# An edge-gated graph layer on one core: transposed h loaded for two row blocks in one transfer, projected rows stored in one transfer of 4 KB packets

## The chip, the core and the metric

The kernel runs on one NeuronCore of a Trainium2 chip. The metric is the time of one execution on the device in microseconds (us), as the median of several runs. A kernel is a program for five engines that run side by side: TensorE (PE, matmuls; its weight loads are PEld), VectorE (DVE), ScalarE (ACT), GpSimd (POOL) and SyncE (SP), which does nothing but hand transfers to the core's 16 DMA engines. They are tied together by semaphores.

## The reference

With B = 16 graphs, N = 1024 nodes and D = 256 features, and one matrix `adj` that serves as both `A_a` and `A_m`:

```python
pre_u = einsum('bud,dk->buk', h, W1[:d]);  pre_v = einsum('bvd,dk->bvk', h, W1[d:])
hidden = relu(pre_u[:, :, None, :] + pre_v[:, None, :, :] + b1)
S   = sigmoid(einsum('buvk,ko->buvo', hidden, W2)[..., 0] + b2)
a_t = einsum('buv,bud->bvd', S * adj, h)
m_t = einsum('uv,bud->bvd', adj, h) * h
z   = beta1 * h + beta2 * (a_t @ Wa + ba) + beta3 * (m_t @ Wm + bm)
```

About 0.9% of `adj` is not zero (some nine entries in a column), so the kernel computes the gate S for these edges alone.

## The kernel before

The 16 graphs are four groups g of four graphs. The 1024 target nodes v are eight row blocks vt of 128. One block of the main loop is a pair (g, vt): 32 blocks, each of T = 10 steps, so 320 steps in all. In a step, 128 edge slots are worked on for the four graphs of g:

- POOL gathers for each slot one row of a table in HBM (`fetched<-table,uidx`, L512). A table row holds, for source node u and the group's four graphs, `pre_u` (1024 floats, the projected row) and beside it h itself (1024 floats), 8 KB together. There is one table per group. A gather takes one of eight places `fetched`, and is issued as soon as TensorE has used the step that was in that place.
- PE spreads `pre_v + b1` to the slots (`pc<-X,mark`, L621), DVE adds it (L652, one instruction a step, by which steps are counted in the trace) and forms the gate's sum (L659, four a step), ACT applies the sigmoid and scales, PE sums over the edges (L675).
- Every block ends with products with Wa and Wm (L746) and two stores of the result, `out_dram<-z` (L753; 256 KB each, 1 KB packets).

Beside this, the tables of the next groups are made while the current group runs. For each row block (g, nt) to come, SP copies h into the table's right half (`copy_h`, L404; 512 KB, 1 KB packets), and loads the transposed h, `hT` (L399; 512 KB, in packets of 512 bytes, since 128 nodes of one feature lie side by side). Then TensorE multiplies it with W1's upper half in two halves (`half_product`, L410), ACT copies each half to SBUF, and SP stores it to the left half of the table (L438; two stores of 256 KB, 2 KB packets). The two halves are made five steps apart: for (2, i) at steps 69+10i and 74+10i, for (3, i) at 149+10i and 154+10i. The same `hT` is read again when the block (g, nt) runs itself, for `pre_v` and for z, and its place is given back only then.

Places for `hT`: eight slices of one tile `wide` (they hold group 0 at the start), two tiles of their own, and from step 71 three more. `pending` lists the loads by the step at which the row block is needed; `made_rows` hands over the first of the list when a place is free and that step is at most AHEAD = 14 steps away. Row blocks (1, 6) and (1, 7) are loaded twice, since group 1's table begins with them (the list `again`; the second time for steps 130 and 140).

The order on every engine is the order of the code (the schedule is manual). SP's transfers are numbered over eight completion semaphores in turn, and each hand-over waits until the transfer eight before it has landed. Nothing can overtake on SP: a store that waits for ACT holds up the load behind it.

Of the kernel before, what the change touches and what calls it, by code (L numbers as in the profile page):

```python
# [7 lines left out]
FP = mybir.dt.float32  # L8
# [5 lines left out]
P = 128  # L14
# [3 lines left out]
def kernel(  # L18
# [42 lines left out]
    nc = tc.nc  # L61
    B, N, D = x.shape
    NT = N // P
    DC = D // P
    GB = 4
    NG = B // GB
    GD = GB * D
# [16 lines left out]
    table = [dram.tile([N, 2 * GD], FP, name=f"table{g}") for g in range(NG)]  # L84
    adj_flat = adjT.rearrange("v (u one) -> (v u) one", one=1)
    x_rows = x.rearrange("b n d -> n b d")
    xT_rows = xT.rearrange("b (c p) n -> p (b c) n", p=P)
# [6 lines left out]
    def load_weights(src, name, engine=nc.scalar):  # L94
        t = const.tile([P, DC, D], FP, name=name)
        engine.dma_start(t, src.rearrange("(c p) k -> p c k", p=P))
        return t
# [102 lines left out]
    big = main.enter_context(tc.tile_pool(name="big", bufs=2))  # L200
# [9 lines left out]
    def small(name):  # L210
        return psm.tile([P, 512], FP, name="misc")
# [158 lines left out]
    def after(step, f):  # L370
        due.setdefault(step, []).append(f)
# [6 lines left out]
    again = [(1, vt) for vt in range(NT - TWICE, NT)]  # L378
    hTs = {}
    NH = NT + 2  # L380

    def hT_places(pool, n, first=0):
        return [pool.tile([P, GB, DC, P], FP, name=f"hT{first + i}") for i in range(n)]

    wide = hts.tile([P, GB, DC, N], FP, name="wide")
    hT_free = hT_places(hts, NH - NT)
    flat = list(hT_free)

    def drop_hT(k, step=None):
        t = hTs.pop(k)  # L390
        if step is None:
            hT_free.append(t)
        else:
            after(step, lambda: hT_free.append(t))

    def load_hT(k, engine=nc.sync):
        g, nt = k
        hTs[k] = hT_free.pop(0)
        engine.dma_start(hTs[k].rearrange("p b c n -> p (b c) n"),  # L399
                         xT_rows[:, g * GB * DC:(g + 1) * GB * DC, nt * P:(nt + 1) * P])  # L400

    def copy_h(k, engine=nc.scalar):
        g, nt = k
        engine.dma_start(table[g][nt * P:(nt + 1) * P, GD:].rearrange("n (b d) -> n b d", b=GB),  # L404
                            x_rows[nt * P:(nt + 1) * P, g * GB:(g + 1) * GB, :])

    def half_product(p, hT, wt, h, begun):
        for bb in range(2):
            for i in range(DC):
                nc.tensor.matmul(p[:, bb * D:(bb + 1) * D], hT[:, 2 * h + bb, i, :], wt[:, i, :],  # L410
                                 start=(i == 0 and not begun), stop=(i == DC - 1), skip_group_check=begun)
# [7 lines left out]
    def copied(step, t, p):  # L419
        if ROOM <= step < BS * T - 4 and step % T in BEHIND or step == BS * T - 7:  # L420
            behind.append((t, p))
        else:
            nc.scalar.copy(t, p)  # L423

    def rows(k, tab=None):

        g, nt = k
        for h in range(2):
            step = yield
            c = slice(2 * h * D, (2 * h + 2) * D)  # L430
            p = small("p")
            half_product(p, hTs[k], w_u, h, False)
            t = big.tile([P, 2 * D], FP, name=f"tab{h}") if tab is None else tab[:, c]
            copied(step, t, p)
            if h == 1 and k in again:
                drop_hT(k, step + 1 if tab is None else None)
            if tab is None:
                after(step + 1, lambda t=t, c=c: nc.sync.dma_start(table[g][nt * P:(nt + 1) * P, c], t))  # L438
        if tab is not None:
            after(step + 1, lambda: nc.sync.dma_start(table[g][nt * P:(nt + 1) * P, :GD], tab))  # L440

# [41 lines left out]
    def do(step):  # L485
        for f in due.pop(step, ()):
            f()

    def go(gen, step):

        try:
            gen.send(step)
        except StopIteration:
            pass
# [2 lines left out]

    BS = NG * NT
    EVS = 3
    ROOM, MORE, LISTS, AHEAD = 10, 3, 70, 14  # L500
    BEHIND = (5, 6, 7, 8)
    APART, minus = 24, []

# [19 lines left out]
    tabs = [fetched[0][:, :GD], fetched[NF - 1][:, :GD], *(f[:, GD:] for f in fetched)]  # L523
    for nt in range(NT):
        hTs[0, nt] = wide[:, :, :, nt * P:(nt + 1) * P]
    for b in range(GB):
        nc.sync.dma_start(wide[:, b], xT_rows[:, b * DC:(b + 1) * DC, :])
        for vt in ((), (0, 1), (2,), (3,))[b]:
            next(made[vt])
# [15 lines left out]
    def load_mark(q):  # L545
        marks[q] = big.tile([P, E], FR, name="mark")
        nc.scalar.copy(marks[q], whose[:, order[q // NW][1] * NW + q % NW, :])
# [17 lines left out]
    for t, turns_ in enumerate(script):  # L565
        step = t - 100
        do(step)
        for c in turns_.split():
            if c == "r":
                k = turn[m % NT]  # L570
# [45 lines left out]
    def expand(n):  # L616
        k, g, vt, w, j = where(n)
        pcs[n] = psc.tile([P, GD], FP, name="pc")
        for h in range(2):
            c = slice(2 * h * D, (2 * h + 2) * D)  # L620
            nc.tensor.matmul(pcs[n][:, c], marks[n // TW][:, j * P:(j + 1) * P], cuts[k][w][:, c],  # L621
                             start=True, stop=True)
# [21 lines left out]
    def fill(n, gap=True):  # L644
        for r in running:
            if r[1] == gap and r[2] <= n:
                piece_of(r, n)
                break

    def add(n):  # L650
        t = fetched[at_slot[n]][:, :GD]
        nc.vector.tensor_tensor(t, t, pcs.pop(n), ALU.add)  # L652
# [109 lines left out]
    def tail_rows(t, v, m, f):  # L762
        g, vt = order[BS - 1]
        for i in range(P // m):
            b = g * GB + i + (f * P // m if m == W else 0)
            yield hbs[BS - 1][i * m:(i + 1) * m, f, :], t[b, vt * P + v:vt * P + v + m, :]
# [37 lines left out]
    at, pending = {}, []  # L804
# [14 lines left out]
    def made_rows(n):  # L819
        nonlocal piece, last  # L820
        while pending and (pending[0][1] in hTs or hT_free and pending[0][0] - (AHEAD if n >= T else 6) <= n):
            k = pending.pop(0)[1]
            if k not in hTs:
                load_hT(k, nc.sync)
        if n in at:
            if at[n] != last:
                last = at[n]
                copy_h(last, nc.sync)
                piece = rows(last)
                next(piece)  # L830
            go(piece, n)
# [46 lines left out]
    def pair_ends():  # L878
        while ends:
            pair_end(ends.pop(0))  # L880
# [3 lines left out]
    def gather_to(last_in):  # L884
        nonlocal done
        while done < min(last_in, total):
            gather_in(done)
            done += 1

    for n in range(total - 3):  # L890
        k, s = divmod(n, T)
        if n < ROOM:
            gather_to(n - 1)
        pair_ends()
        if n % TW == (n < ROOM) and n // TW + 1 < total // TW:
            load_mark(n // TW + 1)
        expand(n + 2)
        if n >= ROOM:
            fill(n, False)
        products(n, k, s)  # L900
        if n >= ROOM and n % 2 == 0:
            gather_to(n)
        add(n + 1)
        gate(n)
        while behind:
            nc.scalar.copy(*behind.pop(0))  # L906
        do(n)
        if n == 0:
            for i in advance[0]:
                next(made[i], None)  # L910
            next(made[EARLY])
            load_hT(turn[NT + 1])
            w_a, w_m = load_weights(Wa, "w_a", nc.sync), load_weights(Wm, "w_m", nc.sync)
            after(10, scale_weights)
        if n == total - 6:
            hbs[BS - 1] = next(t for t in hT_free if t in flat).rearrange("p b c n -> p b (c n)")
            for v, m, f in tails:
                for h, o in tail_rows(x, v, m, f):
                    nc.sync.dma_start(h, o)
        for i in advance.get(n, ()) if n else ():  # L920
            next(made[i], None)
        if n in start_list:
            running.append([made[start_list[n]], True, n])
            piece_of(running[-1], n)
        if n < ROOM:
            fill(n, False)
        if n == LISTS:
            assert not running and all(next(x, None) is None for x in made)
            lists_done()
            more = main.enter_context(tc.tile_pool(name="more", bufs=1))  # L930
            flat.extend(hT_places(more, MORE, NH))
            hT_free.extend(flat[-MORE:])
            minus.append(more.tile([P, P], FR, name="minus"))
            nc.vector.tensor_scalar(minus[0], ident, -1.0, None, ALU.mult)

    k, n = BS - 1, total - 3
# [45 lines left out]
    with tc.If(any_left > 0):  # L982
        with ExitStack() as s2:
# [4 lines left out]
            for vt in range(NT):  # L988
# [17 lines left out]
                f = fb.tile([P, 2 * GD], FP, name="fb_f")  # L1006
# [83 lines left out]
```

## Time and profile before

| | |
|---|---|
| runs | 1022.89, 1018.49, 1019.88 us; median 1019.88 us |
| profiled execution | 1017.41 us; span of its instructions 1015.6 us; granted TensorE clock 0.979 of full speed on average |
| share of the span | PE 94%, PE weight loads 69%, DVE 93%, ACT 87%, POOL 43% |
| transfers | 126622 packets, 373.95 MB, 368 GB/s on average |
| issued by SP, largest | 32 copies of h to the tables, 62 stores of z, 48 stores of projected rows, 26 loads of hT by L399 |

"Span" is the time from the first to the last instruction of the profiled execution. The shares say in which part of it an engine was busy. The page gives the DMA engines' work as the time that packets took, as a share of 16 engines over the span, by queue: q0 are POOL's gathers, q1 is what SP hands over.

### The profile page before, as it was taken

How to read it: one execution, taken by the hardware profiler on the slowest of the kernel's cores; microseconds unless marked ns; L12 is line 12 of the kernel's file. 1: busy time of each engine (PE TensorE's matmuls, PEld its weight loads, DVE VectorE, ACT ScalarE, POOL GpSimd, SP SyncE). 2: the span in 40 equal slices, each digit the busy share in tenths (PEclk: the TensorE clock that was granted, in tenths of full speed). 3: DMA queues.
4: the chain of work that ended last, by engine and by line, in shares of the span. 5: the costliest groups of instructions: out<-in, count | busy, mean ns of one | idle time of the engine just before them, and what ended most of it. 6: DMA issues, size and time to landing. Idle time of an engine off the chain costs nothing.

```text
span 1015.6 us, 21650 instructions
## 1 busy us (share of the span) xinstructions
PE 954.2 (94%) x6408; PEld 702.7 (69%) x6408; DVE 948.0 (93%) x3302; ACT 888.6 (87%) x2754; POOL 436.6 (43%) x441
## 2 busy tenths in 40 slices
PE   7878998988989999999799999999999999999996
PEld 5755766766767777777577777777777776666763
DVE  7589998989889999999889999999999999999994
ACT  3667988888979999999789999999999999999983
POOL 3166766556464334343333434333333344434430
PEclk9988998999999999999999999999999999999998
DMA  9899999889899999999999999999999999999992
GB/s 325 308 345 391 382 319 352 324 293 390 304 382 381 417 409 411 402 402 400 386 366 397 417 410 407 399 404 411 379 409 373 380 374 357 381 366 376 373 362 62
DMA packets 126622, 373.95 MB, mean 368 GB/s; under 512 B 17584, under 2 KB 81072, under 8 KB 90288
## 3 DMA queue, kind: packets, MB, share of 16 engines
q0 software_dynamic: 48640, 296.70, 74.6%
q1 hardware_dynamic: 77232, 75.26, 22.1%
q8 instruction: 53, 0.87, 0.3%
q10 hardware_dynamic: 624, 0.52, 0.2%
q14 instruction: 73, 0.60, 0.2%
HBM read 376.48 MB, written 50.33 MB: 420 GB/s over the span
## 4 chain that ended last, share of the span: by engine, by line
PE 59%; DVE 21%; ACT 6%; issue 6%; DMA 5%; another core or an unknown queue 0%; POOL 0%; SPq 0%; DVEq 0%; POOLq 0%
PE misc L410 18%; PE misc L746 11%; PE pc L621 11%; DVE fetched L659 11%; PE acc L675 10%; DVE fetched L652 8%; PE misc L697 5%; DMA wide<-in_xT_dram 4%; ACT left L666 2%; PE misc L730 2%; DVE LT L714 1%; PE misc L414 1%; DMA fetched<-table,uidx 1%; ACT X L906 1%; ACT ev L683 1%
## 5 line engine op out<-in xcount | busy, mean ns | idle before, releaser
L512 POOL DMA_INDIRECT fetched<-table,uidx x320 | 339.4, 1061 | 502.7 <-PE acc L675 372.4
L659 DVE SCALAR_TENSOR_TENSOR fetched<-fetched,w_b 128x256 f32<-128x256 f32 x1280 | 473.3, 418 | 0.0
L652 DVE TENSOR_TENSOR fetched<-fetched,pc 128x1024 f32<-128x1024 f32 x320 | 388.1, 1213 | 32.6 <-PE pc L621 22.8
L666 ACT ACTIVATE left<-left,gt 128x16 f32<-128x16 f32 x1280 | 285.9, 299 | 0.0
L621 PE MATMUL pc<-X,mark 128*128 128x512 f32 x640 | 228.8, 452 | 15.1 <-issue 7.4
L675 PE MATMUL acc<-fetched,left 128*32 128x256 f32 x2560 | 181.9, 387 | 5.0 <-issue 2.3
L621 PEld LDWEIGHTS pc<-X,mark 128*128 128x128 f32 x640 | 107.3, 190 | 97.9 <-issue 58.6
L675 PEld LDWEIGHTS acc<-fetched,left 128*32 128x32 f32 x2560 | 70.9, 109 | 79.9 <-issue 26.0
L746 PE MATMUL misc<-w_m,LT 128*128 128x256 f32 x496 | 117.6, 380 | 0.0
L746 PE MATMUL misc<-w_a,LT 128*128 128x256 f32 x496 | 117.4, 379 | 0.0
L662 ACT ACTIVATE gt<-sc,b_b 128x4 f32<-128x4 f32 x320 | 96.8, 302 | 13.8 <-DVE fetched L659 10.3
L746 PEld LDWEIGHTS misc<-w_a,LT 128*128 128x128 f32 x496 | 93.6, 189 | 14.3 <-ACT LT L423 0.2
L410 PE MATMUL misc<-w_u,wide 128*128 128x256 f32 x352 | 88.3, 402 | 15.2 <-DMA wide<-in_xT_dram 7.5
L683 ACT COPY ev<-acc 128x512 f32<-128x512 f32 x160 | 92.4, 577 | 11.1 <-remote 3.2
L353 POOL DMA_INDIRECT val<-in_adjT_dram,vidx x80 | 86.9, 1086 | 32.8 <-issue 20.8
L659 DVE DVE_READ_ACCUMULATOR fetched<-fetched,w_b 128x1 f32 x1280 | 100.9, 79 | 0.0
L629 ACT ACTIVATE left<-onehot,val 128x32 f32<-128x32 bf16 x320 | 100.3, 313 | 0.0
L746 PEld LDWEIGHTS misc<-w_m,LT 128*128 128x128 f32 x496 | 89.4, 190 | 10.1 <-issue 0.4
L697 PE MATMUL misc<-ident,ev 128*128 128x128 f32 x642 | 84.3, 276 | 9.7 <-ACT ev L683 4.3
L410 PE MATMUL misc<-w_v,wide 128*128 128x256 f32 x368 | 90.5, 390 | 0.0
L410 PEld LDWEIGHTS misc<-w_u,wide 128*128 128x128 f32 x352 | 70.0, 202 | 27.9 <-issue 8.1
L697 PEld LDWEIGHTS misc<-ident,ev 128*128 128x128 f32 x642 | 74.9, 142 | 20.7 <-ACT ev L683 5.2
(160 smaller groups left out, 996.4 us busy)
## 6 DMA issues: line engine op xcount, KB each, us to landing
table<-in_x_dram SPq DMA_DIRECT2D x32, 512.0 KB
out_dram<-z SPq DMA_DIRECT2D x62, 256.0 KB
table<-tab SPq DMA_DIRECT2D x48, 256.0 KB
wide<-in_xT_dram SPq DMA_DIRECT2D x15, 512.0 KB
hT<-in_xT_dram SPq DMA_DIRECT2D x11, 512.0 KB
fetched<-table,uidx POOLq DMA_INDIRECT x320
wide<-in_xT_dram SPq DMA_DIRECT2D x4, 1024.0 KB
table<-fetched SPq DMA_DIRECT2D x8, 512.0 KB
```

Of the source, the lines that this page charges most:

```text
L410: nc.tensor.matmul(p[:, bb * D:(bb + 1) * D], hT[:, 2 * h + bb, i, :], wt[:, i, :], start=(i == 0 and not begun), stop=(i == DC - 1), skip ...
L512: nc.gpsimd.indirect_dma_start(out=fetched[at_slot[n]], out_offset=None, in_=table[g], in_offset=bass.IndirectOffsetOnAxis(ap=uidx[:, vt * ...
L621: nc.tensor.matmul(pcs[n][:, c], marks[n // TW][:, j * P:(j + 1) * P], cuts[k][w][:, c], start=True, stop=True)
L629: nc.scalar.activation(lefts[n][:, 1::GB, :], onehot[:, vt * NW + w, j, :].unsqueeze(1).to_broadcast([P, GB // 2, V]), AF.Copy, scale=val[ ...
L652: nc.vector.tensor_tensor(t, t, pcs.pop(n), ALU.add)
L659: nc.vector.scalar_tensor_tensor(t[:, b, :], t[:, b, :], 0.0, w2_b, ALU.max, ALU.mult, accum_out=sc[:, b:b + 1])
L662: nc.scalar.activation(gt, sc, AF.Sigmoid, bias=b2_b)
L666: nc.scalar.activation(lefts[n][:, 2 * b, :], lefts[n][:, 1 + b // 2 * GB, :], AF.Copy, scale=gt[:, b:b + 1])
L675: nc.tensor.matmul(accs[i][b * 2 * V:(b + 1) * 2 * V, r, :], left[:, 2 * b - b % 2:2 * b - b % 2 + 2].rearrange("p k v -> p (k v)"), f[:, ...
L683: nc.scalar.copy(evs[i], accs.pop(i))
L697: nc.tensor.matmul(pt[:, :, FROM[j]:FROM[j] + V], evs[i][:, r, c * P:(c + 1) * P], ident, is_transpose=True, start=(j == of[0]), stop=True ...
L746: nc.tensor.matmul(pz[:, bb * D:(bb + 1) * D], LT[:, 2 * h + bb, i if bb else 1 - i, c, :], wt[:, c, :], start=(i == 1 and bb == 0 and c = ...
```

## The change

1. A twin is a tile whose two halves are two neighbouring places. The four neighbouring pairs of `wide` are twins, and of the three places added at step 71 two become one tile `both`, a fifth twin. Where the first load in `pending` has an even nt (and belongs to group 2 or 3, or is (1, 6)), and a twin is wholly free, `load_pair` loads (g, nt) and (g, nt+1) in one transfer of 1 MB, in packets of 1 KB.
2. Where no twin is free, such a load is put off (`break`) until SINGLE = 9 steps before its row block is needed, rather than 14, and is then a single load. What stands behind it in `pending` is put off with it.
3. `free_single` picks the place of a single load so that whole twins stay free if possible.
4. `rows` makes both halves of a projected row block in one tile `tab`, and stores it after the second half in one transfer of 512 KB in packets of 4 KB. For groups 2 and 3 the first half so leaves five steps later than before.

```diff
+    def load_pair(k, two):
+        g, nt = k
+        full = with_twin(two[0])
+        for i, t in enumerate(two):
+            hT_free[:] = [f for f in hT_free if f is not t]
+            hTs[g, nt + i] = t
+        nc.sync.dma_start(full.rearrange("p b c n -> p (b c) n"),
+                          xT_rows[:, g * GB * DC:(g + 1) * GB * DC, nt * P:(nt + 2) * P])
...
     def rows(k, tab=None):
         g, nt = k
+        own = tab is None
+        if own:
+            tab = big.tile([P, GD], FP, name="tab")
         for h in range(2):
             step = yield
             c = slice(2 * h * D, (2 * h + 2) * D)
             p = small("p")
             half_product(p, hTs[k], w_u, h, False)
-            t = big.tile([P, 2 * D], FP, name=f"tab{h}") if tab is None else tab[:, c]
-            copied(step, t, p)
+            copied(step, tab[:, c], p)
...
-            if tab is None:
-                after(step + 1, lambda t=t, c=c: nc.sync.dma_start(table[g][nt * P:(nt + 1) * P, c], t))
-        if tab is not None:
-            after(step + 1, lambda: nc.sync.dma_start(table[g][nt * P:(nt + 1) * P, :GD], tab))
+        after(step + 1, lambda: nc.sync.dma_start(table[g][nt * P:(nt + 1) * P, :GD], tab))
...
+    for nt in range(0, NT, 2):
+        twins.append((wide[:, :, :, nt * P:(nt + 2) * P], (hTs[0, nt], hTs[0, nt + 1])))
...
         while pending and (pending[0][1] in hTs or hT_free and pending[0][0] - (AHEAD if n >= T else 6) <= n):
-            k = pending.pop(0)[1]
+            t, k = pending[0]
+            other = next((e for e in pending if e[1] == (k[0], k[1] + 1)), None)
+            if k not in hTs and other and k[1] % 2 == 0 and (k[0] > 1 or k in again):
+                two = free_pair()
+                if two is None and t - SINGLE > n:
+                    break
+                if two is not None:
+                    load_pair(k, two)
+                    pending.remove(other)
+            pending.pop(0)
             if k not in hTs:
                 load_hT(k, nc.sync)
...
-            flat.extend(hT_places(more, MORE, NH))
-            hT_free.extend(flat[-MORE:])
+            flat.extend(hT_places(more, MORE - 2, NH))
+            hT_free.extend(flat[2 - MORE:])
+            both = more.tile([P, GB, DC, 2 * P], FP, name="both")
+            twins.append((both, (both[:, :, :, :P], both[:, :, :, P:])))
+            hT_free.extend(twins[-1][1])
```

In the built program only SP's order differs, apart from the names of the tiles. Of the 26 loads of hT, 22 stay single; the two pairs are (2,2)+(2,3) into `both` and (2,4)+(2,5) into `wide`. The 48 stores of halves become 24.

SP around steps 110 to 130, before. `hT_203` is the load of row block (2,6), `hT_204` the second one of (1,7), `wide` that of (2,7); the two copies `table_62<-in_x_dram` are those of (2,4) and (2,5):

```order
L404 DMA table_62<-in_x_dram 128x4x256
L438 DMA table_62<-tab_5176 128x512
L399 DMA hT_203<-in_xT_dram 128x8x128
L438 DMA table_62<-tab_5339 128x512
L399 DMA hT_204<-in_xT_dram 128x8x128
L753 DMA out_dram<-z 128x2x256 x2
L404 DMA table_62<-in_x_dram 128x4x256
L438 DMA table_62<-tab_5542 128x512
L399 DMA wide<-in_xT_dram 128x8x128
```

The same place now; the first copy is that of (2,4) again, and the store before the results' stores is (2,4)'s:

```order
L471 DMA table_62<-tab 128x1024
L786 DMA out_dram<-z 128x2x256 x2
L436 DMA table_62<-in_x_dram 128x4x256
L403 DMA hT_203<-in_xT_dram 128x8x128
L403 DMA hT_204<-in_xT_dram 128x8x128
L403 DMA wide<-in_xT_dram 128x8x128
L471 DMA table_62<-tab 128x1024
```

The load of (2,6) moved down past the second half of (2,4), two stores of z and the copy of h for (2,5); the three loads stand next to each other, and that of (2,7) stands ahead of the store it was behind. (The load of (1,6), which was ahead of these rows, stands just above them now, since (2,5) came in a pair.)

SP in group 3's loads, before: the copies of h for (3,0), (3,1), and after each a load, here of (3,2) and (3,3):

```order
L404 DMA table_63<-in_x_dram 128x4x256
L438 DMA table_63<-tab_6637 128x512
L399 DMA wide<-in_xT_dram 128x8x128
L438 DMA table_63<-tab_6800 128x512
L753 DMA out_dram<-z 128x2x256 x2
L404 DMA table_63<-in_x_dram 128x4x256
L438 DMA table_63<-tab_7002 128x512
L399 DMA wide<-in_xT_dram 128x8x128
```

The same two loads now, (3,2) into `wide` and (3,3) into `hT_3755`, in the second of these two blocks:

```order
L436 DMA table_63<-in_x_dram 128x4x256
L471 DMA table_63<-tab 128x1024
L786 DMA out_dram<-z 128x2x256 x2
L436 DMA table_63<-in_x_dram 128x4x256
L403 DMA wide<-in_xT_dram 128x8x128
L403 DMA hT_3755<-in_xT_dram 128x8x128
L471 DMA table_63<-tab 128x1024
```

The load of (3,2) moved back by one block of the loop, from behind (3,0)'s first half to behind the copy of h for (3,1); it stands nine steps ahead of its use. So it goes with (3,0), (3,4) and (3,6).

More of the change, by code (lines that the diff above doesn't have):

```diff
@@ L385, with with_twin @@
     wide = hts.tile([P, GB, DC, N], FP, name="wide")
+    twins = []
+    def with_twin(t):
+        return next((full for full, two in twins if t is two[0] or t is two[1]), None)
     hT_free = hT_places(hts, NH - NT)
@@ L397, in load_hT, with free_pair, free_single, free_pair_all @@
         g, nt = k
-        hTs[k] = hT_free.pop(0)
+        hTs[k] = free_single(k)
         engine.dma_start(hTs[k].rearrange("p b c n -> p (b c) n"),
                          xT_rows[:, g * GB * DC:(g + 1) * GB * DC, nt * P:(nt + 1) * P])
+    def load_pair(k, two):
[6 more added lines that the diff above has]
+                          xT_rows[:, g * GB * DC:(g + 1) * GB * DC, nt * P:(nt + 2) * P])
+    def free_pair():
+        for _, two in twins:
+            if all(any(t is f for f in hT_free) for t in two):
+                return two
+    def free_single(k):
+        mate = hTs.get((k[0], k[1] ^ 1))
+        for _, two in twins:
+            if mate is not None and any(mate is t for t in two):
+                for i, t in enumerate(hT_free):
+                    if any(t is w for w in two):
+                        return hT_free.pop(i)
+        whole_ = free_pair_all()
+        i = next((i for i, t in enumerate(hT_free) if not any(t is w for w in whole_)), 0)
+        return hT_free.pop(i)
+    def free_pair_all():
+        return [t for _, two in twins if all(any(t is f for f in hT_free) for t in two) for t in two]
     def copy_h(k, engine=nc.scalar):
@@ L432, in rows @@
             half_product(p, hTs[k], w_u, h, False)
-            t = big.tile([P, 2 * D], FP, name=f"tab{h}") if tab is None else tab[:, c]
-            copied(step, t, p)
+            copied(step, tab[:, c], p)
             if h == 1 and k in again:
-                drop_hT(k, step + 1 if tab is None else None)
-            if tab is None:
-                after(step + 1, lambda t=t, c=c: nc.sync.dma_start(table[g][nt * P:(nt + 1) * P, c], t))
-        if tab is not None:
-            after(step + 1, lambda: nc.sync.dma_start(table[g][nt * P:(nt + 1) * P, :GD], tab))
+                drop_hT(k, step + 1 if own else None)
+        after(step + 1, lambda: nc.sync.dma_start(table[g][nt * P:(nt + 1) * P, :GD], tab))
     cuts = {}
@@ L499 @@
     EVS = 3
-    ROOM, MORE, LISTS, AHEAD = 10, 3, 70, 14
+    ROOM, MORE, LISTS, AHEAD, SINGLE = 10, 3, 70, 14, 9
     BEHIND = (5, 6, 7, 8)
```

## The prediction

> **What bounds the kernel now.** I read the page first: busy shares, slices, queues.
>
> ```profile
> span 1015.6 us, 21650 instructions
> PE 954.2 (94%) x6408; PEld 702.7 (69%) x6408; DVE 948.0 (93%) x3302; ACT 888.6 (87%) x2754; POOL 436.6 (43%) x441
> DMA  9899999889899999999999999999999999999992
> q0 software_dynamic: 48640, 296.70, 74.6%
> q1 hardware_dynamic: 77232, 75.26, 22.1%
> ```
>
> Three engines are nearly full, and so are the DMA engines: the gathers (q0) take 74.6% of their time and SP's transfers (q1), the only ones that the change touches, 22.1%. Which of them sets the pace differs by stretch, so I cut the span into windows (length, then busy time of PE, PEld, DVE, ACT, POOL with counts, granted clock, DMA share, GB/s).
>
> ```profile
> 450.00:500.00 50.00, 50.00 (x351) 37.45 (x349) 49.84 (x167) 48.12 (x154) 18.37 (x19) 1.00 1.01 391
> 500.00:515.00 15.00, 7.66 (x37) 5.63 (x37) 5.86 (x21) 5.11 (x16) 1.60 (x3) 0.77 1.02 378
> 560.00:610.00 50.00, 50.00 (x351) 37.73 (x350) 49.69 (x163) 48.20 (x153) 18.97 (x19) 1.00 1.03 413
> 760.00:960.00 200.00, 194.51 (x1371) 140.06 (x1362) 199.85 (x699) 190.70 (x632) 83.76 (x77) 1.00 0.98 373
> ```
>
> From 300 to 990 us PE and DVE are busy throughout (49.7 to 50.0 of 50), with DMA shares of 0.98 to 1.03. So the engines set the pace and the DMA keeps up with nothing to spare. The one exception is 500 to 515, where PE works 7.66 of 15 us. The waits of 480 to 530 say why, and the timeline shows the rows (start, length, idle time before).
>
> ```profile
> DVE fetched L652 <- PE pc L621: 9.6, 2, 8.5
> PE misc L410 <- DMA wide<-in_xT_dram: 7.3, 1, 7.3
> 471.93 1.89 PE L410 MATMUL misc<-w_u,hT 128*128 128x256 f32 x8
> 507.38 3.75 PE L410 MATMUL misc<-w_u,wide 128*128 128x256 f32 x8 [7.34 <-DMA wide<-in_xT_dram]
> 511.82 1.22 DVE L652 TENSOR_TENSOR fetched<-fetched,pc 128x1024 f32<-128x1024 f32 x1 [8.54 <-PE pc L621]
> 515.45 1.22 DVE L652 TENSOR_TENSOR fetched<-fetched,pc 128x1024 f32<-128x1024 f32 x1 [1.02 <-PE pc L621]
> ```
>
> By the order of the code the row at 507.38 is row block (2,7), and the one at 471.93 is (2,6). (2,7) came 7.34 us late and cost DVE 8.54 + 1.02 = 9.56 us: a late load costs its lateness plus about 2.2 us. Why it was late is in SP's timeline, where a long row is a hand-over that waited.
>
> ```profile
> 425.17 0.58 SPq L404 DMA_DIRECT2D table<-in_x_dram  x1
> 425.84 7.60 SPq L438 DMA_DIRECT2D table<-tab  x1
> 433.54 2.85 SPq L399 DMA_DIRECT2D hT<-in_xT_dram  x1
> 436.48 13.89 SPq L438 DMA_DIRECT2D table<-tab  x1
> 450.47 0.37 SPq L399 DMA_DIRECT2D hT<-in_xT_dram  x1
> 450.94 16.53 SPq L753 DMA_DIRECT2D out_dram<-z  x2
> 467.52 3.15 SPq L404 DMA_DIRECT2D table<-in_x_dram  x1
> 470.77 0.68 SPq L438 DMA_DIRECT2D table<-tab  x1
> 471.55 7.00 SPq L399 DMA_DIRECT2D wide<-in_xT_dram  x1
> 558.35 6.12 SPq L753 DMA_DIRECT2D out_dram<-z  x2
> 564.52 0.56 SPq L404 DMA_DIRECT2D table<-in_x_dram  x1
> 579.30 4.50 SPq L438 DMA_DIRECT2D table<-tab  x1
> 586.29 6.13 SPq L753 DMA_DIRECT2D out_dram<-z  x2
> 663.12 1.78 SPq L438 DMA_DIRECT2D table<-tab  x1
> 691.09 2.91 SPq L438 DMA_DIRECT2D table<-tab  x1
> 707.60 3.01 SPq L438 DMA_DIRECT2D table<-tab  x1
> ```
>
> (2,7) is the `wide` row: handed over by 478.55, landed by 507.38, so it took 28.8 us, for 512 KB. From 425 on SP waits at nearly every step: its queue is backlogged. After 515 hand-overs are short again; there a block of ten steps lasts 27.9 us (from 558.35 to 586.29). So the kernel's one DMA stall is a deadline missed by the load queue, and the change must be judged by deadlines.
>
> **The change part by part.** *Price of a packet.* Windows of the DMA view give packets, MB and share of 16 engines: the first two rows are 350 to 480, the third is 770 to 980 (stores of z alone, 1 KB packets), the last 440 to 507.4.
>
> ```profile
> q0 software_dynamic: 6727, 42.92, 80.5%
> q1 hardware_dynamic: 11759, 9.57, 21.8%
> q1 hardware_dynamic: 4352, 4.20, 5.7%
> q1 hardware_dynamic: 5479, 4.28, 19.1%
> ```
>
> 21.8% of 130 us on 16 engines, over 11759 packets, is 38.6 ns for 814 bytes on average; 5.7% of 210 us over 4352 is 44.0 ns for 965 bytes. The slope is 0.036 ns a byte and 9 ns a packet are left (7 to 12 by rounding; with the page's average, 22.1% over 77232, 46.5 ns for 974 bytes, nothing is left: bounds 0 and 12). With 9 ns, in time of all 16 engines: a load of hT (1024 packets of 512 bytes) 1.76 us, a pair 2.94 for both, a copy of h 1.47, a store of z 0.73, a half row 0.66, a whole row 1.25.
>
> *Fewer packets.* 24 row blocks save 128 packets each, two pairs 1024 each: 5120 packets, 2.9 us of DMA time (0 to 3.8). It is gained nowhere directly: DVE is busy beside it (49.84 of 50). I take 0; were the DMA the bound, -2.9.
>
> *The load of (2,6).*
>
> ```profile
> 441.46 1.20 DVE L652 TENSOR_TENSOR fetched<-fetched,pc 128x1024 f32<-128x1024 f32 x1
> ```
>
> The row is the start of block 12. Before, between the landings of (2,6) and (2,7) the queue served, in SP's order: a half row, the second (1,7), two z, a copy of h, a half row and (2,7) itself, 0.66 + 1.76 + 1.47 + 1.47 + 0.66 + 1.76 = 7.8 us. At q1's share, 19.1 to 21.8%, that is 36 to 41 us, so (2,6) landed 466 to 471, just ahead of its use at 471.93, which agrees with the absence of a wait there. Now there stand ahead of it also the second half of (2,4), two z and (2,5)'s copy of h: 0.66 + 1.47 + 1.47 = 3.6 us; saved are two pairs and five rows, 2688 packets, 1.5 us. Net +2.1 us, at 21.8% 9.6 us later: 476 to 481. I take 479, late by 7, cost 7 + 2.2 = +9.2. Bounds: with nothing saved +3.6 us, 16.5 us later, up to 16 late, +18; and the queue empty when the load is handed over (the copy of h is handed over 2.3 us after a block's start, as 564.52 + 0.56 is after 562.78, a row quoted below; 441.5 + 2.3 = 444), 444 + 28.8 = 473, late by 1, or less by the next rival. I take the ledger since it reproduces the use at 471.93.
>
> *The load of (2,7).* Handed over with (2,6), not 34 us later, and only 3.5 us of loads behind it; PE's wait at (2,6) lets the queue run. Needed about 500, it lands by 490: the stall goes, -9.6 (bound: 0).
>
> *Group 3's singles.* (3,0), (3,2), (3,4), (3,6) are now handed over behind the copy of h of the block before their use: for (3,2) at 564.52 + 0.56 = 565.1, and PE uses it at 593.25 (the DVE row is the first step of that block).
>
> ```profile
> 562.78 1.21 DVE L652 TENSOR_TENSOR fetched<-fetched,pc 128x1024 f32<-128x1024 f32 x1
> 593.25 1.89 PE L410 MATMUL misc<-w_u,wide 128*128 128x256 f32 x8
> ```
>
> The lead is 28 us; before it was 53 (a load stands one block earlier). Ahead in the queue from 558.35 on: two z, a copy, the load, 4.7 us, at 21.5% (21.8 and 19.1 bracket it) 22 us: landed at 580, 13 us early, if the queue was empty; with the last pair's second load and a row left over, 3.0 us, at 594, late by 1. So hidden, narrowly; with the cover gone each costs 1 + 2.2. The last, (3,6) at step 200, is worse off: SP's waits grow from 1.78 to 3.01 us from 663 to 707. I take one late load, 2 us: +4 (bounds 0, and 4 x 5 = +20).
>
> *Stores of rows.* Each now leaves with its second half, five steps (14 us) later. Who waits: the tile is written again two blocks on, 14 steps (39 us) after the hand-over, and the next group gathers 11 steps (30 us) after its last row. The longest transfer seen is 28.8 us. Cost 0; if a store took 10 us more, ACT would wait that long.
>
> *SP's queue.* 26 hand-overs fewer, and none moved behind a new wait but the loads above. Before step 70 only stores merge, and no wait there is for them: 0, with 2 us either way.
>
> *Sum.* -9.6 + 9.2 + 4 = +3.6 us on the profiled 1017.41 (span 1015.6 and 1.8 around it): 1021.0. The median shown, 1019.88, is 2.5 above that execution, so **1023.5**. From no change I can tell 0.5%, about 5 us: this is within it.
>
> **Rivals.** *1. The stall goes and none comes (faster).* If the two queues take turns packet by packet, what counts is the number of turns. Beside a gather packet (80.5% of 130 us on 16 engines over 42.92 MB, 320 ns for 8 KB) a 512-byte packet's turn lasts 347 ns, so a load's 64 turns on an engine last 22 us, and a pair's 64 turns 23 us for both. The two pairs save some 42 us of turns ahead of (2,6); two z, a copy and a half row cost 27. It lands 15 us earlier than before, though not before 444 + 22 = 466: in time. Then 1019.9 - 9.6 = 1010. The Trainium skill's page DMA: Bandwidth & Descriptors, under Queues, rings and completion order, says that each DMA engine goes round robin between its queues a packet at a time. The row of 350 to 480 is against turns as the limit: 11759 packets of q1 beside 42.92 MB of gathers, 5239 of 8 KB, so q1 got over two packets for each gather packet; it lives on what the gathers leave over. By that rule 1010, by the row's shares 1023.5.
>
> *2. Several singles late (slower).* Nine steps' lead, 28 us, is just what a load took when the queue was backlogged (28.8). If each block of two loads, 2 x 1.76 + 1.47 + 1.47 + 1.25 = 7.7 us against some 6.0 (21.5% of 27.9), begins with over 3 us left over, three of the four come 1 to 4 us late: 3 x 5 = +15 in place of my +4, so 1034. For it: DMA shares of 1.03. Against: after 515 SP hardly waits.
>
> *3. Nothing moves.* (2,6) in time by a hair, (2,7) late as before, group 3 hidden: 1019.9.
>
> **How the numbers follow.** My forecast 0.45: 1019 to 1029, of which 0.30 within 0.5% and 0.15 slower. Rival 1: 0.22, of which 0.19 faster. Rival 2: 0.25, slower. Rival 3: 0.08, same. Together faster 0.19, same 0.41, slower 0.40. The range goes from rival 1 to rival 2: 1009 to 1034; the likeliest case alone 1019 to 1029.
>
> **What would show it.** Right: no PE wait at the row block of step 139 (`wide`), one on `hT` of 5 to 12 us at step 129, DVE's gap there 2 us longer, and a short one near step 209; q1 with 5120 packets fewer and its share near 21.8%. Wrong: no wait on a load after 300 us (rival 1), three or more (rival 2), ACT waiting for a store of `tab`, or POOL's gathers at steps 160 or 240 for a row.

## The result, and the profile after

The changed kernel takes 1033.52 us (median of 4 runs, 1030.48 to 1034.61) against 1019.46 us of the kernel before (4 runs, 1018.49 to 1022.89): a ratio of 1.0119, 95% interval 1.0084 to 1.0154. It is slower by about 1.2%. The forecast was 1023.5; the measured time is near the 1034 of its second rival (several singles late). Ratios leave out a run that is over 1.5% above the fastest one of its kernel (two below, one of them of the kernel before). The profiled execution took 1034.27 us, with a span 16.8 us longer than before. Lines of its page:

```profile
span 1032.4 us, 21574 instructions
PE 959.9 (93%) x6408; PEld 705.2 (68%) x6408; DVE 948.6 (92%) x3302; ACT 888.7 (86%) x2754; POOL 439.4 (43%) x441
DMA  9899989989899999999996999999999999999992
q0 software_dynamic: 48640, 296.70, 73.6%
q1 hardware_dynamic: 71696, 75.25, 21.5%
```

The engines do the same work as before in a longer span. q1 has 5536 packets fewer, as the change says: 5120 of data, and by the packet records 416 of 4 bytes, 16 for each of the 26 transfers saved (24 stores and two loads). The slice in which the DMA engines are only 60% busy (542 to 568 us) shows where to look. The waits of 480 to 630 us (us in total, how often, the longest):

```profile
DVE fetched L685 <- PE pc L654: 19.8, 5, 12.4
PE misc L442 <- DMA wide<-in_xT_dram: 15.2, 2, 11.0
```

Two loads are late where one was. The timeline of after has, in order, the add of step 70, the products of (2,6) and (2,7), then two groups of a late product and the DVE waits behind it:

```profile
308.75 1.21 DVE L685 TENSOR_TENSOR fetched<-fetched,pc 128x1024 f32<-128x1024 f32 x1
478.79 1.03 PE L442 MATMUL misc<-w_u,hT 128*128 128x256 f32 x4
506.73 0.81 PE L442 MATMUL misc<-w_u,wide 128*128 128x256 f32 x3
545.88 0.77 PE L442 MATMUL misc<-w_u,wide 128*128 128x256 f32 x1 [11.04 <-DMA wide<-in_xT_dram]
550.52 1.22 DVE L685 TENSOR_TENSOR fetched<-fetched,pc 128x1024 f32<-128x1024 f32 x1 [12.44 <-PE pc L654]
554.23 1.22 DVE L685 TENSOR_TENSOR fetched<-fetched,pc 128x1024 f32<-128x1024 f32 x1 [1.10 <-PE pc L654]
608.44 1.08 PE L442 MATMUL misc<-w_u,wide 128*128 128x256 f32 x2 [4.14 <-DMA wide<-in_xT_dram]
612.59 1.22 DVE L685 TENSOR_TENSOR fetched<-fetched,pc 128x1024 f32<-128x1024 f32 x1 [4.81 <-PE pc L654]
616.22 1.22 DVE L685 TENSOR_TENSOR fetched<-fetched,pc 128x1024 f32<-128x1024 f32 x1 [1.03 <-PE pc L654]
```

TensorE does not wait for (2,6) or (2,7). The late ones are (3,0), used in step 149, and (3,2), in step 169. In the trace of before, step 70 was here:

```profile
302.69 1.21 DVE L652 TENSOR_TENSOR fetched<-fetched,pc 128x1024 f32<-128x1024 f32 x1
```

So the span's 16.8 us come out as 6.1 before step 70 (308.75 - 302.69), minus the 9.6 of the old stall, plus 12.44 + 1.10 for (3,0) and 4.81 + 1.03 for (3,2): 15.9; 0.9 is left over. SP's timeline shows how the two loads became late:

```profile
450.74 1.83 SPq L403 DMA_DIRECT2D hT<-in_xT_dram  x2
452.70 21.62 SPq L403 DMA_DIRECT2D wide<-in_xT_dram  x1
474.43 10.96 SPq L471 DMA_DIRECT2D table<-tab  x1
506.05 4.76 SPq L436 DMA_DIRECT2D table<-in_x_dram  x1
510.91 10.09 SPq L403 DMA_DIRECT2D wide<-in_xT_dram  x1
576.05 0.58 SPq L403 DMA_DIRECT2D wide<-in_xT_dram  x1
```

The three loads that the change put next to each other, (2,6), the second (1,7) and (2,7), are the first two rows; the third of them takes 21.62 us to be handed over (12.7 us with the shorter queue of the last experiment). (3,0), the row at 510.91, then takes 10.09 us (0.4 us in that experiment). It is handed over by 521.00 and has landed when TensorE starts at 545.88: 10 us of hand-over and 24.9 us of flight, while it was needed at 534.84. (3,2) takes 0.58 us, is handed over by 576.63 and lands at 608.44, 31.8 us later; it was needed at 604.30. By the packet records SP's queue moved nothing at all between 550.8 and 566.7 us, so nothing that was handed over before 562 lay ahead of (3,2).

A transfer ends with 16 packets of 4 bytes, as many as there are DMA engines, which count up its semaphore. For (3,0) the trace has all 16 of these updates: the first at 526.32, eleven by 533.71, so before the load was needed, and the last at 545.75. Read as one for each engine, they say that the load waited for its slowest engines. For (2,7) in the trace of before, late by 7.34 us, eleven of the 13 that are recorded came by 490.99 and the last two at 501.93 and 507.25.

### The profile page after: what moved, and what is told of

Its sections match the earlier page's. It is cut to its first block, busy times and chain, and to the rows that moved or that the text cites. A ratio compares the mean times of both kernels' runs of the same rounds, so it can differ in the third digit from the quotient of the medians.

```text
span 1032.4 us, 21574 instructions
## 1 busy us (share of the span) xinstructions
PE 959.9 (93%) x6408; PEld 705.2 (68%) x6408; DVE 948.6 (92%) x3302; ACT 888.7 (86%) x2754; POOL 439.4 (43%) x441
## 4 chain that ended last, share of the span: by engine, by line
PE 56%; DVE 20%; ACT 9%; DMA 7%; issue 6%; another core or an unknown queue 1%; SPq 0%; DVEq 0%; ACTq 0%
PE misc L442 16%; PE misc L779 11%; PE pc L654 10%; DVE fetched L692 10%; PE acc L708 9%; DVE fetched L685 7%; DMA wide<-in_xT_dram 6%; PE misc L730 4%; ACT left L699 2%; PE misc L763 1%; ACT ev L716 1%; PE misc L446 1%; DVE LT L747 1%; DMA fetched<-in_adjT_dram 1%; ACT gt L695 1%
## 5 line engine op out<-in xcount | busy, mean ns | idle before, releaser
L708 PE MATMUL acc<-fetched,left 128*32 128x256 f32 x2560 | 184.5, 388 | 9.4 <-issue 3.6
L442 PE MATMUL misc<-w_u,wide 128*128 128x256 f32 x352 | 91.3, 412 | 24.0 <-DMA wide<-in_xT_dram 15.3
L692 DVE DVE_READ_ACCUMULATOR fetched<-fetched,w_b 128x1 f32 x1280 | 98.2, 77 | 0.0
L730 PEld LDWEIGHTS misc<-ident,ev 128*128 128x128 f32 x642 | 74.5, 142 | 22.1 <-ACT ev L716 5.0
L442 PE MATMUL misc<-w_v,wide 128*128 128x256 f32 x352 | 85.7, 387 | 0.0
```

What stands on the lines that cost most here:

```text
L692: nc.vector.scalar_tensor_tensor(t[:, b, :], t[:, b, :], 0.0, w2_b, ALU.max, ALU.mult, accum_out=sc[:, b:b + 1])
L708: nc.tensor.matmul(accs[i][b * 2 * V:(b + 1) * 2 * V, r, :], left[:, 2 * b - b % 2:2 * b - b % 2 + 2].rearrange("p k v -> p (k v)"), f[:, ...
L730: nc.tensor.matmul(pt[:, :, FROM[j]:FROM[j] + V], evs[i][:, r, c * P:(c + 1) * P], ident, is_transpose=True, start=(j == of[0]), stop=True ...
```

## The experiments

Four theories for the lost time. A: the loads that are put off cost the 19 us, the merged stores the 6 us. B: the merged stores cost both. C: the 6 us are scatter. D: the pairs cost it all. Four kernels take the change apart; the kernel before had 1017.96 us beside them (29 runs, all but one from 1012.16 to 1023.26).

**stores_only**: the kernel before with the hunk of `rows` from the diff.

> The kernel before, with the merged store of a row block's 4 KB rows and nothing else changed: every load keeps its old step. In the changed kernel 6.1 us were lost before step 70, where only the stores differ, and 19 us at the loads of (3,0) and (3,2). Theory A (the put-off loads cost the 19 us, the merged stores the 6 us): 6 us lost before step 70, the wait for (2,7) still there (7 us or a little less), no wait for a load after step 145: 1022 to 1026. Theory B (the merged stores, which leave 14 us later and fill the queue when it is already late, cost it all): waits of 4 us or more at step 149 or 169 here too, 1035 or more. Theory C (the 6 us are scatter between executions, the stores cost nothing): 1017 to 1020.

1018.98 us (12 runs), ratio 1.0015, 0.9991 to 1.0039. Its trace has the old stall and no other, and step 70 at 302.7, where the kernel before had it:

```profile
506.81 0.77 PE L410 MATMUL misc<-w_u,wide 128*128 128x256 f32 x1 [5.34 <-DMA wide<-in_xT_dram]
```

Merged stores cost nothing and bring nothing that can be measured. B falls, and for the stores C holds.

**loads_only**: the changed kernel without that hunk.

> The changed kernel with the two half stores of before: pairs and putting-off stay, at the same steps. Theory A: waits at steps 149 and 169 as in the changed kernel (11 and 4 us), the 6 us before step 70 gone: 1026 to 1029. Theory B (merged stores are the cause): no such waits, 1008 to 1012. Theory C: as the changed kernel, 1031 to 1035.

1026.95 us (12 runs), ratio 1.0081, 1.0055 to 1.0106. Waits in its trace from 450 to 740:

```profile
PE misc L442 <- DMA wide<-in_xT_dram: 6.8, 2, 3.9
PE misc L442 <- DMA hT<-in_xT_dram: 4.4, 1, 4.4
```

The late ones here are (2,6), (3,2) and (3,6), not (3,0): the cause stays without the merged stores, the place moves. Step 70 is at 308.5 here, so the 6 us are not the stores'. The time lies in theory A's range, but the waits at step 149 and the gain before step 70, from which A had it, did not come: that match is luck.

**not_put_off**: the changed kernel with

```diff
-    ROOM, MORE, LISTS, AHEAD, SINGLE = 10, 3, 70, 14, 9
+    ROOM, MORE, LISTS, AHEAD, SINGLE = 10, 3, 70, 14, 14
```

> The changed kernel with SINGLE = 14, so that no single is put off: the two pairs stay at steps 75 and 95 and all other loads are at the steps of before, stores merged. Theory A: no wait for a load at steps 139, 149 and 169, only the 6 us of the early steps are lost against before and the 9.6 us of the old stall gained: 1014 to 1018. Theory B (stores): waits at 149 or 169 stay, 1025 or more. Theory D (pairs, whose 1024 packets of 1 KB stand in the queue before the rest, cause the late loads): as the changed kernel, 1030 to 1035.

1016.69 us (12 runs), ratio 0.9998, 0.9974 to 1.0021. No load is late, and the time lies in theory A's range, as it said. But the 9.6 us of the old stall are not gained, for a wait that no theory had:

```profile
554.86 1.17 POOL L543 DMA_INDIRECT fetched<-table,uidx  x1 [11.84 <-DMA table<-in_x_dram]
562.76 1.22 DVE L685 TENSOR_TENSOR fetched<-fetched,pc 128x1024 f32<-128x1024 f32 x1 [6.89 <-DMA fetched<-table,uidx]
```

POOL could not issue the first gather of group 2 (step 160), since group 2's table was not complete. The page names the copy of h. By the semaphores that POOL waits for, that copy landed at 550.91 and the last merged row, whose store took from 529.24 to 547.49 to be handed over, at 553.92.

**put_off_only**: the changed kernel without pairs.

```diff
-                two = free_pair()
+                two = None
```

> The changed kernel without pairs: every load is a single, and those with an even nt are still put off to 9 steps before their use ((2,2) at step 80, (2,4) at 100), stores merged. Theory A: the waits at 149 and 169 stay (4 us or more each) and, since 2048 packets more stand in the queue of group 2, waits at (2,2), (2,4), (2,6) or (2,7) come too: 1035 to 1055. Theory D (pairs are the cause): the waits at 149 and 169 go, and the time is near that of before, 1018 to 1026.

1029.31 us (6 runs), ratio 1.0129, 1.0071 to 1.0187, below the range of A and above that of D. PE waits 11.2 us at (2,6) and 2.15 at (3,2):

```profile
PE misc L442 <- DMA wide<-in_xT_dram: 13.3, 2, 11.2
```

Putting off is slow without any pair, so D falls; A's places and sizes were off.

Now two questions: does a gain of the pairs vanish at step 160 because the merged store leaves later (theory S), or because SP's queue has more to serve from step 70 to 160 than it gets, so that something there must be late (theory P)? And does each put-off load pay, or the bunch at step 120 (theory Q)? The kernel before had 1022.49 us beside the next four (28 runs).

**pairs_only**: pairs, nothing put off, two half stores.

> The kernel before with the two pairs at steps 75 and 95 and nothing else: no load put off, two half stores a row block as before. The kernel with pairs and merged stores, without putting-off, lost 6.9 us at step 160, where POOL waited 11.8 us for a copy of h before it could issue the first gather of group 2. Theory P (SP's queue has more packets to serve between steps 70 and 160 than it gets turns, so something at the end of this stretch is late whatever is merged): a wait of 4 us or more at step 139, 149 or 160 here too, 1013 to 1020. Theory S (the merged store of the last row block, which leaves 5 steps later, held the gather back): with half stores no wait over 2 us after 310 us, 1005 to 1011.

1020.93 us (12 runs), ratio 0.9990, 0.9962 to 1.0018; just above P's range, and the kernel before was 4.5 us slower here than beside the first four. The same wait as in not_put_off, now for a half row, which rules out S:

```profile
554.48 0.99 POOL L544 DMA_INDIRECT fetched<-table,uidx  x1 [11.74 <-DMA table<-tab]
562.75 1.22 DVE L686 TENSOR_TENSOR fetched<-fetched,pc 128x1024 f32<-128x1024 f32 x1 [7.11 <-DMA fetched<-table,uidx]
```

**after_again**: the changed kernel once more.

> The changed kernel once more, beside the other variants. If merged stores cost 6 us beside pairs and putting-off (1033.5 in 4 runs against 1027.0 without them in 12): 1031 to 1035. If the difference was scatter between sessions: 1026 to 1030.

1031.12 us (11 runs), ratio 1.0091, 1.0057 to 1.0124; loads_only had 1.0081. The time alone lies in the range for merged stores that cost 6 us. But the kernel before was 4.5 us slower too (1022.49 against 1017.96), and as ratios the two are alike within their intervals, so the merged stores don't show here either. Its trace, with the sum of these waits of DVE from 450 to 740 us at the end:

```profile
304.17 1.21 DVE L685 TENSOR_TENSOR fetched<-fetched,pc 128x1024 f32<-128x1024 f32 x1
481.70 0.77 PE L442 MATMUL misc<-w_u,hT 128*128 128x256 f32 x1 [6.90 <-DMA hT<-in_xT_dram]
486.07 1.22 DVE L685 TENSOR_TENSOR fetched<-fetched,pc 128x1024 f32<-128x1024 f32 x1 [8.02 <-PE pc L654]
711.71 0.77 PE L442 MATMUL misc<-w_u,wide 128*128 128x256 f32 x1 [4.27 <-DMA wide<-in_xT_dram]
716.36 1.22 DVE L685 TENSOR_TENSOR fetched<-fetched,pc 128x1024 f32<-128x1024 f32 x1 [5.67 <-PE pc L654]
DVE fetched L685 <- PE pc L654: 15.4, 3, 8.0
```

The same program reaches step 70 4.6 us sooner than in the first trace, and its late loads are (2,6) and (3,6), not (3,0) and (3,2). Which load is late is not a property of the kernel; that some are, is.

**put_off_group2**: only loads of groups 1 and 2 are put off.

```diff
-                if two is None and t - SINGLE > n:
+                if two is None and k[0] < 3 and t - SINGLE > n:
```

> The changed kernel in which only group 2's and the repeated loads are put off ((1,6) at step 111, (2,6) at 120); (3,0), (3,2), (3,4), (3,6) are back at steps 135, 155, 175, 195. Theory A (each put-off load pays by itself, by its 5 steps of lost lead): the waits at 149 and 169 go, one of at most 5 us at step 129 may stay: 1016 to 1022. Theory Q (the loads that are put off in group 2 bunch at step 120, and the queue behind them is late for 40 us): a wait of 5 to 11 us at step 129, 139 or 149 stays, that at 169 goes: 1022 to 1028.

1020.42 us (12 runs), ratio 0.9982, 0.9958 to 1.0006: 10.7 us below after_again, which ran beside it, and level with the kernel before. One wait is left, at (2,6):

```profile
486.43 0.77 PE L442 MATMUL misc<-w_u,hT 128*128 128x256 f32 x1 [9.47 <-DMA hT<-in_xT_dram]
```

So what slows the changed kernel is group 3's putting-off, as A says. The time is in A's range, but the wait of 9.47 us at step 129 is what Q expected, and A had at most 5: put-off loads of group 2 are late too, in place of the old stall and not on top of it.

**small_packets**: the kernel before, with two loads in packets of 256 bytes.

```diff
+        w = P // 2 if k in ((3, 3), (3, 5)) else P
+        for j in range(0, P, w):
+            engine.dma_start(hTs[k].rearrange("p b c n -> p (b c) n")[:, :, j:j + w],
+                             xT_rows[:, g * GB * DC:(g + 1) * GB * DC, nt * P + j:nt * P + j + w])
```

> The kernel before with the loads of (3,3) and (3,5) each split into two transfers of 64 columns: 2048 packets of 256 bytes in place of 1024 of 512, the same bytes. From first to last packet these loads took 17 to 25 us. If a packet takes a turn whatever its size (as the pairs say, whose 1024 packets of 1 KB took 16 to 20 us for twice the bytes): 34 to 50 us. If bytes count and a packet costs 9 ns: 18 to 28 us. The use of (3,3) and (3,5) is 14 steps (39 us) after the hand-over, so by the first a wait of up to 13 us at each, 1018 to 1045; by the second none, 1014 to 1022.

One run, 1018.53 us. By the packet records, the 2048 packets of (3,3) took 22.1 us from first to last and those of (3,5) 25.3, and neither load is late. So a packet does not cost a turn whatever its size. But bytes don't set the time either: from the end of the hand-over to the last recorded update the pairs took 25 to 34 us in the traces of after, not_put_off and pairs_only, and loads of half the bytes, in the same 1024 packets, 23 to 31 us in the trace of before (those handed over between 307 and 480 us). Up to step 165 this program is the kernel before, and yet its stall is at step 160 and not at (2,7):

```profile
555.72 0.99 POOL L514 DMA_INDIRECT fetched<-table,uidx  x1 [10.69 <-DMA out_dram<-z]
563.91 1.22 DVE L654 TENSOR_TENSOR fetched<-fetched,pc 128x1024 f32<-128x1024 f32 x1 [6.05 <-DMA fetched<-table,uidx]
```

(The store of z is named because it shares a semaphore; the last that POOL waited for was a half row, at 554.95.) Even the kernel before has no fixed place for its stall. That is theory P, and its test is to take work out of the stretch (the kernel before: 1022.71 us, 27 runs).

**copies_early**: not_put_off, with four copies of h handed over before step 60. There the DMA engines have some time: their mean share in the trace of before is 0.95 from 115 to 245 us, and 1.03 from 300 to 450.

```diff
+    early = {24: (2, 4), 34: (2, 5), 44: (2, 6), 54: (2, 7)}
...
+        if n in early:
+            copy_h(early[n], nc.sync)
         if n in at:
             if at[n] != last:
                 last = at[n]
-                copy_h(last, nc.sync)
+                if last not in early.values():
+                    copy_h(last, nc.sync)
```

> The kernel with pairs and merged stores and nothing put off, in which the copies of h for (2,4) to (2,7) are handed over at steps 24, 34, 44 and 54 (where the DMA share of before is 0.88 to 0.98) and not at steps 109 to 139. Theory P (SP's queue has more to serve between steps 70 and 160 than it gets, so something at the end of that stretch must be late): with 4 x 1.47 = 5.9 us of DMA time less there, at a share of 21.8% some 27 us of queue, no wait for a load or a row from step 129 to 165; a ratio to before of 0.990 to 0.995 (5 to 10 us faster), less up to 3 us if the early steps pay. Rival E (the end of group 2 waits for one transfer's own lead, not for the queue's length; or the engines have no time to spare anywhere): a wait of 4 us or more stays between steps 129 and 165, or more is lost before step 70: ratio 0.997 to 1.005.

1013.86 us (10 runs), ratio 0.9920, 0.9894 to 0.9946: faster than both kernels. All that is left of waits for transfers from 450 to 740 us:

```profile
DVE fetched L685 <- DMA fetched<-table,uidx: 0.8, 2, 0.5
POOL fetched L543 <- DMA table<-in_x_dram: 0.3, 1, 0.3
```

Step 70 is at 309.73 us here, later than in the trace of before (302.69). It is at 309.88 in copies_on_act, which has no early copies, so a cost of theirs is not shown; the gain is net of it.

**copies_early_before**: the kernel before with the same edit alone.

> The kernel before with only this: the copies of h for (2,4) to (2,7) at steps 24, 34, 44 and 54. If the length of the queue makes the stall (theory P), taking 5.9 us of DMA time out does what pairs and merged stores could not: no wait at steps 139 and 160, ratio 0.990 to 0.996, and the pairs are not needed for it. If the pairs' 2048 packets are needed too: a wait of 1 to 5 us is left, ratio 0.995 to 1.0. Rival E: a wait of 5 us or more stays, ratio 0.998 to 1.005.

1014.89 us (12 runs), ratio 0.9929, 0.9902 to 0.9956. The early copies do it without pairs and merged stores, and these add nothing that can be told (the intervals overlap nearly whole). Its trace is of its slowest execution, 1027.8 us. It has no wait at steps 129 to 160 either. But the load of (3,6) is 8.4 us late at step 209, though it has fourteen steps of lead in the code:

```profile
DVE fetched L652 <- PE pc L621: 11.7, 3, 9.8
PE misc L410 <- DMA wide<-in_xT_dram: 8.4, 1, 8.4
```

So the early copies relieve the stretch up to step 160; they do not rule out a late load behind it. Why SP's queue was late there in this execution is not known.

**copies_on_act**: not_put_off, with the copies of groups 2 and 3 handed over by ACT.

```diff
-                copy_h(last, nc.sync)
+                copy_h(last, nc.scalar if last[0] > 1 else nc.sync)
```

> The kernel with pairs and merged stores and nothing put off, in which the copies of h of groups 2 and 3 are handed over by ACT, on its own DMA queue, at the same steps. If the order within SP's queue is what makes things late (a copy stands between loads), a queue of its own gives the copies turns of their own, and the wait at step 160 goes: ratio 0.990 to 0.996. If the 16 engines' time is what is short between steps 70 and 160, a second queue takes it from the gathers: a wait of 4 us or more stays at step 139 to 165, or DVE waits for gathers before: ratio 0.997 to 1.005.

1021.13 us (12 runs), ratio 0.9991, 0.9961 to 1.0021. The copies go by ACT's queue (q10 on the page, with 624 packets in the kernel before), and no load or row is late in the trace. But ACT, busy 87% of the time, now waits at a hand-over 4.48 us for a store of z to land, and PE and DVE wait for ACT:

```profile
q10 hardware_dynamic: 9072, 8.91, 2.6%
```

```profile
683.89 0.56 ACTq L436 DMA_DIRECT2D table<-in_x_dram  x1
684.54 0.59 ACT L455 COPY tab<-misc 128x512 f32<-128x512 f32 x1 [4.48 <-DMA out_dram<-z]
685.79 0.64 PE L708 MATMUL acc<-fetched,left 128*32 128x256 f32 x1 [2.81 <-ACT left L699]
688.63 1.22 DVE L685 TENSOR_TENSOR fetched<-fetched,pc 128x1024 f32<-128x1024 f32 x1 [4.37 <-PE pc L654]
```

The Trainium skill's page DMA: Bandwidth & Descriptors, under Issuing engines are not separate DMA queues, says that transfers of all engines share the 16 DMA engines, so that a second issuer saves only issuing time. The time agrees. The trace does not settle it: the copies' bytes stayed in the stretch and yet no load or row is late, but ACT's waits came in their place.

Last: does putting off still cost when the queue is short (lead theory), or only when it is long (queue theory)? (The kernel before: 1021.36 us, 17 runs.)

**copies_early_put_off**: the changed kernel with the early copies.

> The changed kernel, pairs, merged stores and putting-off, with the copies of h for (2,4) to (2,7) at steps 24, 34, 44 and 54. If putting off costs only because the queue is already long at steps 111 to 140 (queue theory), the shorter queue makes the four put-off loads of group 3 land in time: no wait at steps 149 to 209, ratio to before 0.990 to 0.996, as without putting-off. If nine steps (25 to 28 us) of lead are too few whatever stands ahead (lead theory), one or two of (3,0) to (3,6) are still 2 to 5 us late, and (2,6) may be: ratio 0.996 to 1.004, some 5 to 10 us above the kernel with early copies and no putting-off.

1023.39 us (12 runs), ratio 1.0020, 0.9985 to 1.0055, as the lead theory said: 1.0% above copies_early, each against the kernel before that ran beside it. In its trace group 2's waits are gone, and group 3's are there:

```profile
562.17 0.60 SPq L403 DMA_DIRECT2D wide<-in_xT_dram  x1
592.80 0.45 PE L442 MATMUL misc<-w_u,wide 128*128 128x256 f32 x1 [2.37 <-DMA wide<-in_xT_dram]
678.22 0.74 SPq L403 DMA_DIRECT2D wide<-in_xT_dram  x1
710.65 0.76 PE L442 MATMUL misc<-w_u,wide 128*128 128x256 f32 x1 [4.15 <-DMA wide<-in_xT_dram]
```

Neither (3,2) nor (3,6) is held up at its hand-over (0.60 and 0.74 us); they land 30.0 and 31.7 us later. Nine steps are too few.

## Why the prediction was right and where not

The range, 1009 to 1034, just held the time, and the slower side was given 0.40; the likeliest case, +3.6 us, was not what happened. That the time fell on rival 2's 1034 is partly luck: rival 2 had (2,6) late for 9.2 and three singles late for 15. The first trace has (2,6) in time, two singles late for 19.4, and 6.1 lost before step 70. In the trace of after_again the forecast's own marks came, all of them: no wait at (2,7), 6.90 us at (2,6), one late single near step 209. Its span is 9.6 us longer than before's. By the steps of the forecast:

- *Fewer packets: 0.* Right: merged stores alone 1.0015, pairs alone 0.9990.
- *The load of (2,7): the stall goes, -9.6.* Right in both traces of the changed kernel, and in vain. The step reads the stall as one load's deadline. The runs point to the overflow of a stretch: with the DMA engines full from step 70 on (a share of 1.01 to 1.03), one wait that costs DVE 6 to 14 us falls between steps 129 and 160 in each of the ten traces without early copies or ACT's queue, at (2,6), (2,7), (3,0) or the gather of step 160. In the first trace the wait drains the queue (nothing moves from 550.8 to 566.7 us).
- *The load of (2,6): late by 7, +9.2.* In after_again it was 6.90 us late and cost 8.02 + 1.01. In the first trace its last recorded update is at 478.4, where the step had 479; it was in time, for a use at 478.79, only because the program ran 6.1 us later. The ledger of the queue is right here, but the term is one form of that one wait, which falls elsewhere in other traces.
- *A late load costs its lateness and 2.2 us more.* 11.04 us cost 13.54, 4.14 cost 5.84: 2.5 and 1.7.
- *Group 3's singles: one load late by 2 us, +4.* This is the term that was mis-sized. Two were late in the first trace and cost 19.4; one, by 4.27, in after_again, and cost 7.4 (15.4 - 8.0). The experiment without them is 10.7 us faster. What failed is the landing "if the queue was empty", worked out from work over share: 22 us from the stores ahead, which is 15 us from the load's own hand-over (565.1 to 580). (3,2) took 31.8 us from there, and 30.0 with the queue relieved, where the lead is 28. Work over share treats the 16 engines as one, but the updates of (3,0) lie 19 us apart. The row at hand, 28.8 us for (2,7), was the better guide, and rival 2 used it. Rival 2's own condition, over 3 us left over from the block before, was not needed.
- *Before step 70: 0, 2 us either way.* The scatter was taken too small: two traces of the same program have step 70 at 308.75 and 304.17. No change of the mean is shown.
- *Stores of rows: 0.* Right, though the next group's first gather, which the step named as the one who waits, turned out to be next in line for the stall.
- *Rival 1* had the stall gone and no other: 1010. That is copies_early (1013.86), reached by taking work out of the stretch and not by the pairs. Its rule from the Trainium skill (DMA: Bandwidth & Descriptors, Queues, rings and completion order) was read too finely: the page's packet holds some 9 to 17 descriptors, and the prediction took it for the profile's packet. 2048 packets beside the gathers in 22.1 and 25.3 us (small_packets), 128 for each engine, are 0.17 to 0.20 us each, not the 0.35 of that reading.

What stays open: why, beside the gathers, a load takes some 20 to 36 us to land, whether in 1024 or 2048 packets and 512 KB or 1 MB, and why the engines finish their shares of it so far apart. No run gave group 3 other leads than nine and fourteen steps.

## What to carry to other kernels

Where the DMA engines are full over a long stretch, one visible stall is the overflow of the whole stretch: here, mending the transfer that is late only moved it, and what helped was to move transfers out of the stretch (four copies, 2 MB in 2048 packets, 0.8%; the pairs save 2048 packets but no bytes, and brought nothing). A transfer that is put off for a better shape pays with its lead; measure the flight there (30 us here, not what its bytes would take) before giving up five steps of it. Loads that were in time before (group 3) lose their lateness in full, while in the full stretch (group 2) the same edit only changes the stall's place. A load landed here with the last of its 16 updates, so the average share of the engines gave its landing too early.

## What was not expected of the hardware

- The same instructions stall in different places from one execution to the next, and 28 runs of the kernel before, beside the second set of experiments, spread from 1015.40 to 1029.92 us; a single trace shows the mechanism, not the place.
- A late load idles the DMA engines as well. In the DMA view of after from 500 to 720 us (40 slices of 5.5 us), the tenth, around 552 us, moves 6 GB/s: by the packet records no gather starts a packet from 544.8 to 555.0 us, and SP's queue moves nothing after 550.8.

```profile
GB/s 418 416 416 427 411 398 398 385 252 6 319 243 411 413 411 408 419 393 398 384 386 258 277 369 379 381 414 392 401 413 412 423 417 413 387 368 413 417 393 403
```
